# Adding a bias to the rows of a graph-attention table instead of to their weighted sums

## The chip, the cores and the metric

The kernel runs on one core of a Trainium2 chip. The metric is the device time of one execution in microseconds. The names of the engines are PE (matrix products; PEld is its loading of weights), DVE (vector), ACT (scalar and activation), POOL (GpSimd, which also issues the indirect gathers) and SP (which issues most of the other transfers).

## The reference

The reference applies a two-layer graph attention network (GAT) to 3125 nodes with 768 features and 53125 edges that are sorted by destination. Cut to what matters:

```python
h = relu(layernorm(x))                       # 3125 x 768
# layer 1: 4 heads of 256 columns
xl = h @ W1                                  # 3125 x 1024, the "table"
e  = leaky_relu((xl . a_src)[src] + (xl . a_dst)[dst])
alpha = softmax of e over the edges of one destination   # sums to 1 per node
out = segment_sum(xl[src] * alpha, dst) + b1
h1 = relu(layernorm(out) * g1 + be1) + h @ Wr1 + br1
# layer 2: the same with 1 head of 768 columns on h1, bias b2; result added to x
```

The attention logits come from `h` and folded weights, not from the stored table. The weights alpha of a node, with that of its own row in the table, add up to 1, so a constant that is added to each row of the table is found in each weighted sum once.

## The kernel before

**Tiling.** The nodes are worked in 25 blocks of 125 (`NB`, `P`). The edges of a block lie in a window of 18 groups (`J`) of 128 edges.

**Products of layer 1.** `products` (L636 to L654) multiplies each block by `w1` in two halves of 512 columns; ACT copies each half from PSUM to a tile `row` (L648; two buffers), and POOL's queue stores the row to the DRAM table `table1` (L146, L147: 112 and 13 rows). Each `yield` after three matmuls is a step that other code calls as filler, in an order that is written out by hand for PE, ACT and DVE. The loads of `x` tiles beyond the fourth go through the same POOL queue (L140), eight blocks ahead of their use.

**Softmax of layer 1.** `softmax` (L333 to L484) looks up the logits with one-hot matrices: per block DVE builds `ohd`, `le`, `ohs` and `ohh` (L375 to L382), PE multiplies `ohs` by small tables `tabs` (L392) and `ohd` by `tabd` (L400), and DVE multiplies and reduces the results (L394, L397, L402). The filler steps of `products` stand between them on PE. The small tables come from a split of the logits into three bfloat16 parts (`part`, `rest`). A scratch tile `scr`, in the place where later `wr1` lies, holds larger intermediates.

**Between softmax and sums.** PE ends the products and multiplies the first four blocks by `wr1` (L744). DVE folds the attention vectors of layer 2 into `wa2` from tiles `ab2`, `w2k` and `w2t` (L736, L737). Then the pools of the sums open in memory that earlier pools have left, and the first use of each tile waits for the last use of what lay there.

**Sums of layer 1.** `sums` (L486 to L571) gathers, for each block, 18 groups of 128 rows of 1024 columns by indirect DMA on POOL's queue (`g`, L525, ten buffers, so up to ten gathers ahead). ACT and DVE split each weighted row into two fp32r parts (`hi` L543, `g` L544), and PE sums them into `pa` through a one-hot matrix `oh` (L548); one group in 18 goes by another form (`w`, L558, L560). At the end of each block two matmuls of two rows (`ones_r` and `bias`, L564) add the bias, which was split into two fp32r parts beforehand by `split_biases` and loaded as `b1_r`. Between the groups PE takes steps of other work: residual products from `h0k` tiles (L777), and `end1` of the block before (L807, L820). Here a scheduler with its own estimates, not the hand, sets the order on the engines.

**Layer 2** goes through the same functions with one head and its own bias `b2`.

Of the kernel before, what the change touches and what calls it, by code (L numbers as in the profile page):

```python
# [9 lines left out]
F32 = mybir.dt.float32  # L10
F32R = mybir.dt.float32r
BF16 = mybir.dt.bfloat16
# [16 lines left out]
J = 18  # L29
# [29 lines left out]
def in_order(  # L59
# [42 lines left out]
    slo16_d = dram.tile([E], I16, name="slo16_d")  # L102
    keep_d = dram.tile([H * NB, S + 2], BF16, name="keep_d")

    parts_d = dram.tile([2, HC + 2 * C2], F32, name="parts_d")

    ident = const.tile([128, 128], F32, name="ident")
    make_identity(nc, ident)
# [45 lines left out]

    def split_biases(pool):

        for name, vec, plus, n, o in (("b1", b1, None, HC, 0), ("b2", b2, None, C2, HC), ("ball", br2, be2, C2, HC + C2)):
            v = pool.tile([128, n // 128], F32, name=name + "_v")
            nc.sync.dma_start(v, vec.rearrange("(p c) -> p c", p=128))
            if plus is not None:  # L160
                u = pool.tile([128, n // 128], F32, name=name + "_u")
                nc.sync.dma_start(u, plus.rearrange("(p c) -> p c", p=128))
                nc.vector.tensor_add(v, v, u)
            hi = pool.tile([128, n // 128], F32R, name=name + "_hi")
            nc.vector.tensor_copy(hi, v)
# [167 lines left out]
    def softmax(heads, asad, al, alo_d, pp, nq, ends=False, scr=None, fill=iter(()), side=None,  # L333
# [8 lines left out]
        with tc.tile_pool(name="so", bufs=1, side=side, reuse_waits=waits) as so:  # L342
            own = so.tile([128, J, V, NB], F32, name="own")
            if scr is not None:
                first = scr()
                n = J * heads * NB
                picks = [first[:, :n].rearrange("p (j h b) -> p j h b", h=heads, b=NB)]
                ohhs = [first[:, n + i * J * NB:n + (i + 1) * J * NB].rearrange("p (j b) -> p j b", b=NB)
                        for i in range(2)]
                le = first[:, n + 2 * J * NB:n + 2 * J * NB + S // 2].bitcast(BF16)  # L350
            with tc.tile_pool(name="sb", bufs=2, side=side, reuse_waits=waits) as sb:

                part = sb.tile([P, 3, NB * V], BF16, name="part", bufs=1)
                rest = sb.tile([P, NB * V], F32, name="rest", bufs=1)
                flat = asad.rearrange("p b v -> p (b v)")
                nc.vector.tensor_copy(part[:, 0, :], flat)
                nc.vector.tensor_sub(rest, flat, part[:, 0, :])
                nc.vector.tensor_copy(part[:, 1, :], rest)
                nc.vector.tensor_sub(part[:, 2, :], rest, part[:, 1, :])
                tabs = sb.tile([P, 3, heads, NB], BF16, name="tabs", bufs=1)  # L360
                tabd = sb.tile([P, NB, 3, V], BF16, name="tabd", bufs=1)
                for i in range(3):
                    v = part[:, i, :].rearrange("p (b v) -> p b v", v=V)
                    nc.vector.tensor_copy(tabs[:, i], v[:, :, :heads].rearrange("p b h -> p h b"))
# [51 lines left out]
            with tc.tile_pool(name="sr", bufs=1, side=side, reuse_waits=waits) as sr:  # L416
# [2 lines left out]
                bw = sr.tile([R, S], F32, name="bw")  # L419
                eo = sr.tile([128, J, heads, NB], F32, name="eo")  # L420
                m = sr.tile([128, J, heads, NB], F32, name="m")
                s = sr.tile([128, J, heads, NB], F32, name="s")
                keep = sr.tile([R, S + 2], BF16, name="keep")
                nc.sync.dma_start(keep, keep_d[:R, :])
                pen = sr.tile([R, S + 2], BF16, name="pen")
# [60 lines left out]
    def sums(heads, cols, table, al, alo_d, bias, split, ahead, his, lag, gp, pp, end, more=iter(())):  # L486
# [4 lines left out]
        f = width // 2  # L491
        n = min(cols, f)
        assert split(0) or n == f
        running = []

        def step():
# [19 lines left out]
        with tc.manual_schedule(engines={PE, ACT, DVE}) if lag else nullcontext():  # L516
            for b in range(NB):
                own = gp.tile([128, width], F32, name="own", bufs=3 if lag else 2)
                pa = pp.tile([P, 2, 512], F32, name="pa", bufs=2)
                ao = gp.tile([128, heads + 1], F32, name="ao", bufs=3)  # L520
                for j in range(J):
                    c = b * J + j
                    g = gp.tile([128, width], F32R, name="g", bufs=ahead)
                    gf = g.bitcast(F32)
                    nc.gpsimd.indirect_dma_start(  # L525
                        out=gf, out_offset=None, in_=table[:, :],
                        in_offset=bass.IndirectOffsetOnAxis(ap=idx_s[:, c:c + 1], axis=0))
                    if j == 6:
                        load_rows(nc.sync, own, table, b)
                    if j == 2:  # L530
                        nc.gpsimd.indirect_dma_start(
                            out=ao, out_offset=None, in_=alo_d[:, :],
                            in_offset=bass.IndirectOffsetOnAxis(ap=at_last[:, b:b + 1], axis=0))
                    if split(j) or heads > 1:
                        oh = gp.tile([128, 128], F32R, name="oh", bufs=max(his, 4) + 4)
                        nc.vector.tensor_scalar(oh, iota_f, rel_s[:, c:c + 1], None, op0=OP.is_equal)  # L536
                    if split(j):

                        hi = gp.tile([128, width], F32R, name="hi", bufs=his)
                        for h in range(heads):  # L540
                            cs = slice(h * cols, (h + 1) * cols)
                            a = al[:, j, h, b:b + 1]
                            nc.scalar.activation(hi[:, cs], gf[:, cs], AF.Copy, scale=a)  # L543
                            nc.vector.scalar_tensor_tensor(g[:, cs], gf[:, cs], a, hi[:, cs].bitcast(F32),  # L544
                                                           op0=OP.mult, op1=OP.subtract)
                        for t in (hi, g):
                            for i in range(2):
                                nc.tensor.matmul(pa[:, i, :f], oh[:, :P], t[:, i * f:(i + 1) * f],  # L548
                                                 start=(j == 0 and t is hi), stop=False)
# [12 lines left out]
                    if j == J - 1:  # L562
                        for i in range(2):
                            nc.tensor.matmul(pa[:, i, :f], ones_r, bias[:, i * f:(i + 1) * f],  # L564
                                             start=False, stop=True)
                    step()
                running.append(finish(b, own, pa, ao))
            while running:
                step()


    with tc.tile_pool(name="m1", bufs=1) as mp:
# [10 lines left out]
        with tc.tile_pool(name="w1", bufs=1) as wp, tc.tile_pool(name="pm1", bufs=1, space=PSUM) as pm1:  # L583
            w1 = wp.tile([128, NK1, HC], F32, name="w1")
            wa1 = wp.tile([128, NK1, 2 * H], F32, name="wa1")
            h0 = []
            with tc.tile_pool(name="d1", bufs=2) as dp, tc.tile_pool(name="pd1", bufs=1, space=PSUM) as pp:
                xts = {}

# [47 lines left out]
                def products():  # L637

                    for b in range(NB):
                        gi, o = b // GB, (b % GB) * P  # L640
                        row = wp.tile([P, HC], F32, name="row", bufs=2)
                        for i in range(2):
                            pm = pm1.tile([128, 512], F32, name="pm", bufs=3)
                            for k in range(NK1):
# [3 lines left out]
                                    nc.scalar.activation(row[:, i * 512:(i + 1) * 512], pm[:P], AF.Copy)  # L648
                                if k % 3 == 2:
                                    if i == 1 and k == NK1 - 1:  # L650
                                        store_rows(nc.gpsimd, table1, b, row)
                                        if gi and (b % GB == GB - 1 or b == NB - 1):
                                            nc.sync.dma_start(h0T_d[gi][:, :, :o + P], h0[gi])
                                    yield  # L654
# [59 lines left out]
                        next(fill)  # L714
            with tc.tile_pool(name="pq1", bufs=1, space=PSUM) as pp:
                softmax(H, asad1, al1, alo1_d, pp, 4, True,
                        lambda: mp.tile([128, 2 * S], F32, tag="wr1", name="scr"), fill=fill, steps=(3, 8, 2, 8, 2))
                br1_c = by_chunk(br1, mp, NK2, "br1_c")
                wr1 = mp.tile([128, NK1, HC], F32, tag="wr1", name="wr1")
                for k in range(NK1):  # L720
# [29 lines left out]
        with tc.tile_pool(name="w2", bufs=1, reuse_waits="tile") as wp, tc.tile_pool(name="e1", bufs=2, reuse_waits="tile") as ep, \  # L750
# [9 lines left out]

            for k in range(NK1):
                load(1, k)
            b1_r = bias_rows(wp, 0, HC, "b1_r")
            g1_c = by_chunk(g1, wp, NK2, "g1_c")
            be1_c = by_chunk(be1, wp, NK2, "be1_c")
            for k in range(NK2):
# [59 lines left out]
                        nc.vector.tensor_copy(asad2[:, b, :], pm[:, 384:n])  # L826
                store_rows(nc.sync, table2, b, row)

            sums(H, C1, table1, al1, alo1_d, b1_r, lambda j: j % 18 != 8, 10, 4, 0, gp, pp, end1, later())


    with tc.tile_pool(name="m2", bufs=1, reuse_waits="tile") as mp, \
            tc.tile_pool(name="pr2", bufs=1, space=PSUM, reuse_waits="tile") as pr:
        al2 = mp.tile([128, J, 1, NB], F32, name="al2")
        ball_r = bias_rows(mp, HC + C2, C2, "ball_r")
        FIRST = 9
        xrs = {}
        loaded = {}
# [60 lines left out]

        with tc.tile_pool(name="w3", bufs=1, reuse_waits="tile") as wp, tc.tile_pool(name="e2", bufs=2, reuse_waits="tile") as ep, \  # L900
                tc.tile_pool(name="g2", bufs=1, reuse_waits="tile") as gp, tc.tile_pool(name="pg2", bufs=1, space=PSUM, reuse_waits="tile") as pp:
            b2_r = bias_rows(wp, HC, C2, "b2_r")
            g2_b = wp.tile([P, C2], F32, name="g2_b")
            nc.sync.dma_start(g2_b, bcast(g2, C2))

# [483 lines left out]
```

## Time and profile before

| | us |
|---|---|
| median of 5 runs | 2362.45 (2352.91 to 2367.83) |
| the profiled execution, its own time | 2356.76 |
| span of its core | 2354.9 |
| PE, DVE, ACT, POOL busy | 2208.5, 1975.4, 1293.9, 1217.0 |

The span is cut into stages by the instructions in it: start and products (0 to about 225), softmax of layer 1 (225 to 464, with products until 468 and `wr1` products until 508), sums of layer 1 (508 to 1507), softmax of layer 2 (to about 1680), sums of layer 2 (to the end). In rows of the timeline the first number is the start, the second the duration or the stretch of several like instructions, and brackets hold the idle time before the first of them with what ended it. A float32 product is recorded as two matmuls, so a pair there is one instruction of the program.

### The profile page before, as it was taken

To read this page: it belongs to the slowest core of one execution; us is meant where nothing else is said; L and a number is where in the kernel's file an instruction comes from. 1 tells how busy PE (TensorE), PEld (TensorE's weight loads), DVE (VectorE), ACT (ScalarE), POOL (GpSimd) and SP (SyncE) were. 2 spreads that over 40 slices of the span, in tenths; PEclk is the share of its full clock that TensorE was granted. 3 is DMA by queue.
4 is the path that set the end of the run, shared out by engine and by line. 5 is a ranking of instruction groups with operands and counts; after the bars stand their busy time and mean duration, and the time that the engine had idled before them with its cause. 6 is when DMAs were issued, how large, how long until landed. Compare 5 with 4: busy or idle time off the path is not lost. (4 is left out here: it accounts for less than half of the span.)

```text
span 2354.9 us, 35889 instructions
## 1 busy us (share of the span) xinstructions
PE 2208.5 (94%) x11154; PEld 1439.7 (61%) x11154; DVE 1975.4 (84%) x4429; ACT 1293.9 (55%) x2687; POOL 1217.0 (52%) x1043
## 2 busy tenths in 40 slices
PE   5898999989999999999999999799999999999996
PEld 2466665446666666666666765466566676666664
DVE  6845999769999999898989999588678788788877
ACT  1231332229988888888888999100244444444443
POOL 2100000027766766566766676000377777777775
PEclk8998999999999999999999999799999999999998
DMA  5453552379998898988988988687499999998996
GB/s 186 154 195 98 187 191 81 114 249 386 326 323 305 294 336 294 312 312 302 324 294 295 337 316 298 232 290 253 154 311 337 322 329 314 329 322 308 305 307 216
DMA packets 185691, 637.97 MB, mean 271 GB/s; under 512 B 32170, under 2 KB 49435, under 8 KB 184724
## 3 DMA queue, kind: packets, MB, share of 16 engines
q0 software_dynamic: 109072, 437.23, 54.1%
q1 hardware_dynamic: 72570, 188.75, 22.9%
q10 hardware_dynamic: 3850, 9.60, 1.1%
q8 instruction: 93, 1.52, 0.3%
q14 instruction: 106, 0.87, 0.1%
HBM read 567.40 MB, written 68.08 MB: 270 GB/s over the span
## 5 line engine op out<-in xcount | busy, mean ns | idle before, releaser
L525 POOL DMA_INDIRECT g<-table,idx_s x900 | 1110.0, 1233 | 464.6 <-PE pa L548 264.2
L543 ACT ACTIVATE hi<-g,al 128x256 fp32r<-128x256 f32 (+1 forms) x2025 | 1008.8, 575 | 462.1 <-DMA g<-table,idx_s 267.5
L544 DVE SCALAR_TENSOR_TENSOR g<-g,al,hi 128x256 fp32r<-128x256 f32 (+1 forms) x2025 | 1033.0, 560 | 125.8 <-ACT hi L543 123.8
L548 PE MATMUL pa<-hi,oh 128*125 128x512 f32 (+1 forms) x1500 | 602.5, 481 | 23.4 <-DVE oh L536 14.2
L548 PE MATMUL pa<-g,oh 128*125 128x512 f32 (+1 forms) x1500 | 472.5, 390 | 22.0 <-DVE g L544 21.9
L548 PEld LDWEIGHTS pa<-hi,oh 128*125 128x125 f32 x1500 | 274.8, 189 | 215.1 <-issue 66.2
L548 PEld LDWEIGHTS pa<-g,oh 128*125 128x125 f32 x1500 | 272.2, 187 | 101.2 <-DVE g L544 58.1
L820 PE MATMUL p<-w,h1T 128*125 128x384 f32 (+1 forms) x800 | 300.1, 494 | 1.8 <-DVE h1T L811 1.5
L854 PE MATMUL pr<-wr,h 128*125 128x384 f32 x800 | 296.6, 503 | 3.1 <-DMA h<-h1T_d 3.1
L645 PE MATMUL pm<-w,h 128*125 128x512 f32 x600 | 281.1, 618 | 0.0
L777 PE MATMUL pr<-h0k,wr 128*128 128x500 f32 (+1 forms) x576 | 257.4, 536 | 8.9 <-DMA h0k<-h0T_d 8.1
L536 DVE TENSOR_SCALAR oh<-iota_f,rel_s 128x128 fp32r<-128x128 f32 x775 | 208.0, 280 | 58.4 <-PE pa L548 58.4
L560 PE MATMUL pa<-g,w 128*125 128x384 f32 (+1 forms) x700 | 234.3, 463 | 5.1 <-ACT w L558 4.1
L854 PEld LDWEIGHTS pr<-wr,h 128*125 128x125 f32 x800 | 151.0, 193 | 86.2 <-issue 14.4
L820 PEld LDWEIGHTS p<-w,h1T 128*125 128x125 f32 x800 | 148.5, 188 | 81.4 <-issue 10.8
L146 POOL DMA_DIRECT2D table<-row x25 | 16.0, 640 | 348.4 <-ACT row L648 321.3
L645 PEld LDWEIGHTS pm<-w,h 128*125 128x125 f32 x600 | 112.9, 196 | 125.3 <-issue 124.0
L560 PEld LDWEIGHTS pa<-g,w 128*125 128x125 f32 x700 | 129.4, 189 | 70.2 <-ACT w L558 12.4
L777 PEld LDWEIGHTS pr<-h0k,wr 128*128 128x128 f32 x576 | 104.5, 191 | 51.9 <-ACT hi L543 6.5
L392 PEld LDWEIGHTS <-ohs 125*128 125x128 bf16 x2700 | 101.6, 98 | 47.9 <-DVE ohs L380 32.9
L392 PE MATMUL pq<-tabs,ohs 125*128 125x100 bf16 (+1 forms) x2700 | 105.2, 193 | 22.3 <-DVE ohs L380 20.5
L648 ACT ACTIVATE row<-pm 125x512 f32<-125x512 f32 x50 | 29.8, 595 | 149.3 <-PE pm L645 138.4
(198 smaller groups left out, 1683.2 us busy)
## 6 DMA issues: line engine op xcount, KB each, us to landing
bd<-dst_d SPq DMA_DIRECT2D x50, 576.0 KB
bs<-slo_d SPq DMA_DIRECT2D x50, 576.0 KB
g<-table,idx_s POOLq DMA_INDIRECT x900, 5.9
r1T_d<-rt SPq DMA_DIRECT2D x100, 125.0 KB
r1t<-r1T_d SPq DMA_DIRECT2D x25, 500.0 KB
h1T_d<-h1T SPq DMA_DIRECT2D x25, 500.0 KB
h<-h1T_d SPq DMA_DIRECT2D x25, 500.0 KB
own<-table SPq DMA_DIRECT2D x24, 512.0 KB
```

The source lines that it names most:

```text
L392: nc.tensor.matmul(q[:, j], ohs[:P, (j0 + j) * 128:(j0 + j + 1) * 128], tabs[:, i], start=(i == 0), stop=(i == 2))
L525: nc.gpsimd.indirect_dma_start(out=gf, out_offset=None, in_=table[:, :], in_offset=bass.IndirectOffsetOnAxis(ap=idx_s[:, c:c + 1], axis=0))
L536: nc.vector.tensor_scalar(oh, iota_f, rel_s[:, c:c + 1], None, op0=OP.is_equal)
L543: nc.scalar.activation(hi[:, cs], gf[:, cs], AF.Copy, scale=a)
L544: nc.vector.scalar_tensor_tensor(g[:, cs], gf[:, cs], a, hi[:, cs].bitcast(F32), op0=OP.mult, op1=OP.subtract)
L548: nc.tensor.matmul(pa[:, i, :f], oh[:, :P], t[:, i * f:(i + 1) * f], start=(j == 0 and t is hi), stop=False)
L560: nc.tensor.matmul(pa[:, o // f, o % f:o % f + n], w[:, o // cols, :], gf[:, o:o + n], start=(j == 0), stop=False)
L645: nc.tensor.matmul(pm[:P], h0[gi][:, k, o:o + P], w1[:, k, i * 512:(i + 1) * 512], start=(k == 0), stop=(k == NK1 - 1))
L648: nc.scalar.activation(row[:, i * 512:(i + 1) * 512], pm[:P], AF.Copy)
L777: nc.tensor.matmul(pm[:, :nb * P], wr1[:, k, m * 128:(m + 1) * 128], loaded[gi, k][:, :nb * P], start=(k == 0), stop=(k == NK1 - 1))
L820: nc.tensor.matmul(pm[:, :n], hT[:, k, :], w2[:, k, o:o + n], start=(k == 0), stop=(k == NK2 - 1))
L854: nc.tensor.matmul(pm[:, :384], h1[:, k, :], wr2[:, k, i * 384:(i + 1) * 384], start=(k == 0), stop=False)
```

## The change

The bias `b1` is loaded once, at the start, by ACT's queue as a tile `b1_b` of 125 equal rows. POOL adds it to each finished `row` before the row is stored to `table1`. The two matmuls of the bias at the end of each block of layer 1's sums go, and with them the preparation and the load of `b1_r`. To make room, `part`, `rest` and `tabd` of layer 1's softmax move into the scratch tile, and `s` shares the buffer of `m`.

```diff
-        for name, vec, plus, n, o in (("b1", b1, None, HC, 0), ("b2", b2, None, C2, HC), ("ball", br2, be2, C2, HC + C2)):
+        for name, vec, plus, n, o in (("b2", b2, None, C2, 0), ("ball", br2, be2, C2, C2)):
...
+                if scr is not None:
+                    part = first[:P, n:n + 3 * NB * V // 2].bitcast(BF16).rearrange("p (i v) -> p i v", i=3)
+                    n += 3 * NB * V // 2
+                    rest = first[:P, n:n + NB * V]
+                    n += NB * V
+                    tabd = first[:P, n:n + 3 * NB * V // 2].bitcast(BF16).rearrange(
+                        "p (b i v) -> p b i v", i=3, v=V)
...
-                s = sr.tile([128, J, heads, NB], F32, name="s")
+                s = m
...
-                                                 start=(j == 0 and t is hi), stop=False)
+                                                 start=(j == 0 and t is hi),
+                                                 stop=(bias is None and j == J - 1 and t is g))
...
-                    if j == J - 1:
+                    if bias is not None and j == J - 1:
...
+            b1_b = wp.tile([P, HC], F32, name="b1_b")
+            nc.scalar.dma_start(b1_b, bcast(b1, HC))
...
                                     if i == 1 and k == NK1 - 1:
+                                        nc.gpsimd.tensor_add(row, row, b1_b)
                                         store_rows(nc.gpsimd, table1, b, row)
...
-                        lambda: mp.tile([128, 2 * S], F32, tag="wr1", name="scr"), fill=fill, steps=(3, 8, 2, 8, 2))
+                        lambda: mp.tile([128, NK1 * HC], F32, tag="wr1", name="scr"), fill=fill, steps=(3, 8, 2, 8, 2))
...
-            b1_r = bias_rows(wp, 0, HC, "b1_r")
...
-            sums(H, C1, table1, al1, alo1_d, b1_r, lambda j: j % 18 != 8, 10, 4, 0, gp, pp, end1, later())
+            sums(H, C1, table1, al1, alo1_d, None, lambda j: j % 18 != 8, 10, 4, 0, gp, pp, end1, later())
```

What the two built programs differ in: on PE 50 instructions are gone and the order of the rest is kept but for the first and the last two blocks of the sums; POOL has 25 more, in four of the first blocks with a load of `x` between the addition and its two stores; SP has four transfers fewer and ACT's queue one more; DVE has two fewer. The places of tiles in on-chip memory also move. Before, the ten `g` buffers of layer 1 lie at bytes 137728 to 178688 of each partition and `ab2` at 172032 to 178176; after, `g` lies at 133536 to 174496 and `ab2` at 176032 to 182176. The second gather of layer 1 waits, before, for the last DVE instruction of the fold that reads `ab2`; after, for the last product of `products`.

More of the change, by code (lines that the diff above doesn't have):

```diff
@@ L103, in in_order @@
     keep_d = dram.tile([H * NB, S + 2], BF16, name="keep_d")
-    parts_d = dram.tile([2, HC + 2 * C2], F32, name="parts_d")
+    parts_d = dram.tile([2, 2 * C2], F32, name="parts_d")
     ident = const.tile([128, 128], F32, name="ident")
@@ L349, in softmax @@
                         for i in range(2)]
-                le = first[:, n + 2 * J * NB:n + 2 * J * NB + S // 2].bitcast(BF16)
+                n += 2 * J * NB
+                le = first[:, n:n + S // 2].bitcast(BF16)
+                n += S // 2
             with tc.tile_pool(name="sb", bufs=2, side=side, reuse_waits=waits) as sb:
-                part = sb.tile([P, 3, NB * V], BF16, name="part", bufs=1)
-                rest = sb.tile([P, NB * V], F32, name="rest", bufs=1)
+                if scr is not None:
[5 more added lines that the diff above has]
+                        "p (b i v) -> p b i v", i=3, v=V)
+                else:
+                    part = sb.tile([P, 3, NB * V], BF16, name="part", bufs=1)
+                    rest = sb.tile([P, NB * V], F32, name="rest", bufs=1)
+                    tabd = sb.tile([P, NB, 3, V], BF16, name="tabd", bufs=1)
                 flat = asad.rearrange("p b v -> p (b v)")
@@ L360, in softmax @@
                 tabs = sb.tile([P, 3, heads, NB], BF16, name="tabs", bufs=1)
-                tabd = sb.tile([P, NB, 3, V], BF16, name="tabd", bufs=1)
                 for i in range(3):
@@ L493, in sums @@
         assert split(0) or n == f
+        assert split(J - 1)
         running = []
@@ L834, in in_order @@
         al2 = mp.tile([128, J, 1, NB], F32, name="al2")
-        ball_r = bias_rows(mp, HC + C2, C2, "ball_r")
+        ball_r = bias_rows(mp, C2, C2, "ball_r")
         FIRST = 9
@@ L901, in in_order @@
                 tc.tile_pool(name="g2", bufs=1, reuse_waits="tile") as gp, tc.tile_pool(name="pg2", bufs=1, space=PSUM, reuse_waits="tile") as pp:
-            b2_r = bias_rows(wp, HC, C2, "b2_r")
+            b2_r = bias_rows(wp, 0, C2, "b2_r")
             g2_b = wp.tile([P, C2], F32, name="g2_b")
```

## The prediction

> **What bounds the kernel now.** I read the page's table of 40 slices first, then the windows view over the stages that the change touches, the PE timeline of one block of the sums, the timeline of the turn from softmax to sums, and DVE and POOL side by side in the softmax.
>
> Busy time by stage, from the windows view (stretch, length, then busy time and instructions of PE, PEld, DVE, ACT, POOL, then clock, DMA share, GB/s):
>
> ```profile
> core 0: us, PE busy (x) PEld busy (x) DVE busy (x) ACT busy (x) POOL busy (x), PEclk, DMA share, GB/s
> 240.00:300.00 60.00, 56.57 (x681) 37.48 (x679) 60.00 (x84) 21.09 (x22) 4.68 (x6) 1.00 0.57 182
> 826.85:866.49 39.64, 39.64 (x143) 25.65 (x142) 36.35 (x100) 34.10 (x86) 27.56 (x19) 1.00 0.94 337
> 600.00:1300.00 700.00, 698.12 (x2501) 451.46 (x2500) 643.54 (x1782) 602.70 (x1502) 468.67 (x339) 1.00 0.90 309
> ```
>
> The sums of layer 1 are bound by PE: it idles 1.9 of 700 us at full clock, while DVE has 3.3 us to spare in a block of 39.64. The softmax of layer 1 is bound by DVE, which idles not at all in 240 to 300, with PE close behind. So the change takes work from the bound of one stage, and puts work beside the bound of another.
>
> One block's end on PE, with the bias pair and, later, the same three neighbours without it:
>
> ```profile
> 826.29 0.63 PE L548 MATMUL pa<-g,oh 128*125 128x512 f32 x2
> 826.85 0.72 PE L564 MATMUL pa<-b_r,ones_r 2*125 2x512 f32 x2
> 827.50 1.56 PE L820 MATMUL p<-w,h1T 128*125 128x384 f32 x4
> 828.60 0.92 PE L548 MATMUL pa<-hi,oh 128*125 128x512 f32 x2
> ...
> 849.25 0.62 PE L548 MATMUL pa<-g,oh 128*125 128x512 f32 x2
> 849.71 1.46 PE L820 MATMUL p<-w,h1T 128*125 128x384 f32 x4
> 850.71 0.92 PE L548 MATMUL pa<-hi,oh 128*125 128x512 f32 x2
> ```
>
> Durations overlap here, so starts are compared: from the start of `g` to the start of the next `hi` it is 2.31 us with the pair and 1.46 without. The pair costs 0.85 us.
>
> The turn to the sums (POOL's gathers; then what PE waits for):
>
> ```profile
> 477.18 1.01 POOL L525 DMA_INDIRECT g<-table,idx_s  x1 [7.36 <-issue]
> 502.63 0.96 POOL L525 DMA_INDIRECT g<-table,idx_s  x1 [24.44 <-DMA r1T_d<-rt]
> ...
> 513.78 3.67 PE L777 MATMUL pr<-h0k,wr 128*128 128x500 f32 x4 [5.68 <-DMA h0k<-h0T_d]
> 521.19 1.11 PE L777 MATMUL pr<-h0k,wr 128*128 128x500 f32 x2 [2.46 <-DMA h0k<-h0T_d]
> ```
>
> The second gather stands still for 24.44 us. The profile names a transfer; the program's waits name the fold of `wa2` on DVE, whose last product starts near 501. Then nine gathers and the loads of `h0k` go out together, the DMA engines are full (share 1.01 in 510 to 520), and PE idles 8.1 us for `h0k`.
>
> DVE and POOL beside each other in the softmax:
>
> ```profile
> 304.13 0.81 DVE L380 TENSOR_SCALAR ohs<-bs,node_f 128x2304 bf16<-128x2304 int16 x1
> 304.32 0.73 POOL L146 DMA_DIRECT2D table<-row  x1 [19.43 <-ACT row L648]
> 304.85 0.62 DVE L382 TENSOR_TENSOR scr<-iota_f,hi_s 128x450 f32<-128x450 f32 x1
> ```
>
> The store's issue takes 0.73 us here, and 0.99 to 1.19 at 245.60, 263.39, 283.21 and 341.67, against 0.53 to 0.54 at 321.85 and 380.31, where DVE is in reductions or in products from PSUM. POOL is held up by some DVE instructions, so the two get in each other's way.
>
> **The bias pair goes.** 24 blocks by 0.85 us, and the first, where no L820 stands behind the pair (551.82 to 553.03, 1.21 against 0.47), 0.75: 21.1 us, all on PE's path. The next limit is near: a block of 38.8 us leaves DVE 2.4 and ACT 4.7, and gathers wait mostly for PE to free buffers (264.2 us by the page). I take 20, between 17 and 21.
>
> **The turn to the sums.** Unasked, the new layout lets gathers 2 to 10 go from about 480 on instead of 502.63, while the DMA engines have room (share 0.62 in 450 to 500). ACT still copies the last residual at 508.13 and takes the first `hi` at 508.71, so nothing starts sooner there; but the loads of `h0k` meet emptier queues, and the first of them no longer waits for PE's last L744. What can go is the 8.1 us of PE idle. What is late next: the second `h0k` load, still issued by SP near 511, and DVE, which needs about 1.87 us for a group (four L544 at 0.41, one `oh` at 0.21). Against it, nine gathers of 512 KB beside the fold's `w2k` loads can hold the fold up; it has 4 us before 508.71. I take 6 off, between 0 and 8.
>
> **The addition on POOL.** 25 instructions of 125x1024 with two inputs; no row shows one. From below, DVE's add of two inputs takes 2026 ns for 1800 columns (L460): 1.15 us for 1024. From above, POOL's nearest row:
>
> ```profile
> masks.py:199 POOL TENSOR_SCALAR_AFFINE_SELECT ident<-ident 128x128 f32<-128x128 f32 x1 | 0.3, 284 | 0.0
> ```
>
> 284 ns for 128 columns, in proportion 2.27 us for 1024. I take the upper, the same engine's. The Trainium skill, "GPSIMD Engine Reference", section "Performance versus the Vector engine", gives 4497 ns for such an add over 2048 columns; half of it is an estimate of 2.25 us, which no run here has shown yet.
>
> As POOL's own time, 25 by 2.27 is hidden: rows come at least 9 us apart and POOL idles 321.3 us for them. Behind the addition its two stores and, early, one load of `x` are queued; the loads are eight blocks ahead, else PE's transposes would wait 2.3 us each. The buffer of `row` is wanted again two blocks later, 20 us at the densest, against 0.6 + 2.3 + 3.8 (landing). The last store goes near 471 instead of 468.78 and the first gather 2.3 us later; ACT needs it only at 508.71.
>
> What is not hidden is what DVE loses. If DVE never waits, 0. If an addition shuts out every DVE instruction that either runs fast on 2304 columns or reads two tiles, I lay 2.27 us at each of the 25 times of L146 over DVE's timeline: between 240 and 410, where each DVE delay moves PE too, six of nine additions block for 2.2 to 2.3 us (245.60, 263.39, 283.21, 304.32, 341.67, 362.78) and two more beside the scans (394.75, 405.06): 18.2 us. With 1.15 us it is 9.3. From 421 to 442 PE is late instead (DVE waits 5.8 us for it at 443), which hides two more. I take 12, nearer to the upper end, since the store issues show the meeting at just these six places, but the phases will shift as PE gains time.
>
> The Trainium skill speaks against this part: "SBUF — State Buffer", section "Who interferes with whom", has DVE and GpSimd share one pair of ports under a lock for the whole instruction, where the second "fully blocks". By it the term would be 18 and the total 6 us higher; the trace shows only POOL as the one that waits.
>
> **The rest.** Before 225 ten additions meet a DVE with gaps: 1, from 0 to 3. The load of `b1_b` (500 KB, at the best slice's 386 GB/s 1.3 us) joins the start, where DVE waits 11.21 us for small bias loads until 32.20; one of these goes: 1, from -1 to 3. SP's four fewer transfers lie where SP is not waited for. `part`, `rest`, `tabd`, and `s` in `m` keep DVE's order, and the scratch tile's next writer comes after PE's last `tabd` product anyway: nothing, and if that order failed, one PE product of 0.6 us.
>
> **Sum.** -20 - 6 + 12 + 1 + 1 = -12 on the profiled execution's 2356.76, so 2344.8. That execution lies 5.7 below the median 2362.45; the median goes to 2350. A measurement of this kernel can tell about 0.5% from no change, 11.8 us; my sum lies just beyond.
>
> **Rivals.** (a) DVE does not wait; POOL alone does, as the store issues show. Then -24: 2338. (b) DVE is blocked in full and the turn gives nothing, because the fold is held up or DVE's pace replaces the idle: -20 + 18 + 2 = 0, 2362. For it: DVE has no idle to absorb anything there. (c) Slower: POOL's two reads follow each other at the one-input row's price, 4.5 us an addition. Over the same timeline this blocks DVE for 38 us between 240 and 410; with -26 and +2 it makes +14, 2376. It decides from about 3.0 us an addition on (24 us of blocking cancel the gain). Against it: 284 ns must contain a fixed part, since a POOL fill of 128x1 already takes 0.10. (d) PE is not the true bound of the sums, since its ends are modelled, and the pair's time goes to waits for DVE: half the gain, 2360. Against it: PE's groups of starts add up without gaps.
>
> **Numbers.** Forecast 0.45, (a) 0.22, (b) 0.20, (c) 0.08, (d) 0.05. The forecast's own range, 2344 to 2356, lies on both sides of the bound, half and half. Faster by over 0.5%: 0.23 + 0.22 = 0.45; within: 0.22 + 0.20 + 0.05, less 0.02, 0.45; slower: (c) and 0.02 for unseen costs on top of the worst sum of bounds (-17 + 18 + 3 + 3 = +7, 2369), 0.10. The best sum is -21 - 8 + 0 + 0 - 1 = -30, 2332. Range 2334 to 2366: it leaves out (c) and the edges of (a) and (b).
>
> **What would show it.** Right: a block of the sums of 38.8 us; the second gather near 480; no 5.68 us before the first L777; DVE rows of L375 to L382 stretched, or gaps before them, beside each POOL addition of about 2.3 us; and the last L744 ending near 522 instead of 508. Wrong: blocks still near 39.6, additions over 3 us, or `al` (L397) ending at the same time as before.

## The result, and the profile after

The changed kernel takes 2373.15 us (median of 42 runs, 2364.88 to 2384.79), against 2363.30 for the kernel before (79 runs on the same chips). The ratio is 1.0043, with a 95% interval of 1.0035 to 1.0051: about 10 us slower, where 12 us faster was predicted. The profiled execution took 2371.62 us with a span of 2369.8. That of before (2356.76) lies 6.5 below the median of its 79 runs, so the two spans differ by 14.9 where the medians differ by 10; below, what the price of a part is comes from ratios times 2363, and what it is made of comes from traces.

Busy time by stage, after, from the windows view (columns as in the prediction; the one block of the sums is 39.00 long):

```profile
240.00:300.00 60.00, 52.81 (x605) 34.11 (x604) 60.00 (x79) 18.99 (x20) 8.28 (x9) 1.00 0.57 183
827.00:866.00 39.00, 39.00 (x142) 25.48 (x141) 36.46 (x102) 33.74 (x86) 27.77 (x21) 1.00 0.97 361
600.00:1300.00 700.00, 699.65 (x2527) 457.62 (x2526) 656.75 (x1825) 614.64 (x1550) 457.89 (x349) 1.00 0.90 317
```

In the softmax DVE is still busy all the time, but in 60 us it now gets through 79 instructions instead of 84, and PE through 605 instead of 681: DVE is not idle, it is slow. In the sums PE is the bound as before.

The end of two blocks on PE, after, from the timeline:

```profile
827.53 0.62 PE L560 MATMUL pa<-g,oh 128*125 128x512 f32 x2
827.99 1.46 PE L836 MATMUL p<-w,h1T 128*125 128x384 f32 x4
...
866.34 0.62 PE L560 MATMUL pa<-g,oh 128*125 128x512 f32 x2
866.80 1.46 PE L836 MATMUL p<-w,h1T 128*125 128x384 f32 x4
```

The pair is gone from between `g` and the products of L836, and the same place comes round after 38.81 us, against 39.64 before.

The turn on POOL, and what PE waits for there, after:

```profile
500.71 2.35 POOL L667 TENSOR_TENSOR row<-row,b_b 125x1024 f32<-125x1024 f32 x1 [6.59 <-ACT row L664]
...
511.91 1.61 POOL L537 DMA_INDIRECT g<-table,idx_s  x1 [7.50 <-issue]
513.83 0.96 POOL L537 DMA_INDIRECT g<-table,idx_s  x1 [0.30 <-issue]
515.10 0.94 POOL L537 DMA_INDIRECT g<-table,idx_s  x1 [0.31 <-issue]
```
```profile
541.43 1.92 PE L793 MATMUL pr<-h0k,wr 128*128 128x500 f32 x4 [1.20 <-DMA h0k<-h0T_d]
```

The second gather no longer stands still (it starts 1.92 us behind the first, where before it was 25.45), and PE's first wait for `h0k` is 1.20 us instead of 5.68. But the last row of the table is added only at 500.71; ACT's first `hi` comes at 541.6, against 508.7 before. Stage 1 (all that lies before the first `hi`) has lost 33 us, where the prediction had 14.

Where: POOL and DVE beside each other, after, from their timelines:

```profile
299.54 2.79 POOL L667 TENSOR_TENSOR row<-row,b_b 125x1024 f32<-125x1024 f32 x1 [17.97 <-ACT row L664]
```
```profile
297.57 2.01 DVE L407 TENSOR_REDUCE al<-scr 128x72 f32<-128x1800 f32 x1
299.51 0.61 DVE L392 TENSOR_TENSOR scr<-iota_f,hi_s 128x450 f32<-128x450 f32 x1
300.04 2.91 DVE L385 TENSOR_SCALAR ohd<-bd,node_f 128x2304 bf16<-128x2304 int16 x1
302.87 1.25 DVE L404 TENSOR_TENSOR scr<-pq,scr 128x500 f32<-128x500 f32 x2
```

L385 takes 0.81 us alone and 2.91 here: it ends 0.6 us after the addition, much as if it had begun behind it. DVE stays "busy" in the table, so no idle time and no wait shows this; only the mean of a group does, or one row beside another engine's. The groups of DVE in 240 to 400, before (the other two of its kind stood at 809 ns there) and then after:

```profile
L375 DVE TENSOR_SCALAR ohd<-bd,node_f 128x2304 bf16<-128x2304 int16 x19 | 15.4, 811 | 0.0
```
```profile
L385 DVE TENSOR_SCALAR ohd<-bd,node_f 128x2304 bf16<-128x2304 int16 x21 | 23.4, 1112 | 0.0
L390 DVE TENSOR_SCALAR ohs<-bs,node_f 128x2304 bf16<-128x2304 int16 x20 | 20.4, 1021 | 0.0
L387 DVE TENSOR_SCALAR scr<-bd,node_f 128x2304 bf16<-128x2304 int16 x19 | 18.2, 960 | 0.0
```

And the addition itself, from its group on the page and from the view of its line (min, median and max in ns):

```profile
L667 POOL TENSOR_TENSOR row<-row,b_b 125x1024 f32<-125x1024 f32 x25 | 66.1, 2645 | 314.1 <-ACT row L664 308.4
```
```profile
L667 POOL TENSOR_TENSOR row<-row,b_b x25: 2339/2349/4534, 46.4 to 500.7; 125x1024 f32<-125x1024 f32 x25
```

Alone it takes 2.35 us. That is what the prediction used (2.27).

### The profile page after: what moved, and what is told of

The parts are those of the page before. It is cut to its first block, busy times and chain, and to the rows that moved or that the text cites. A ratio compares the mean times of both kernels' runs of the same rounds, so it can differ in the third digit from the quotient of the medians.

```text
span 2369.8 us, 35878 instructions
## 1 busy us (share of the span) xinstructions
PE 2201.4 (93%) x11104; PEld 1436.8 (61%) x11104; DVE 2006.0 (85%) x4427; ACT 1286.8 (54%) x2687; POOL 1260.8 (53%) x1068
## 5 line engine op out<-in xcount | busy, mean ns | idle before, releaser
L537 POOL DMA_INDIRECT g<-table,idx_s x900 | 1088.9, 1210 | 444.4 <-PE pa L560 267.4
L836 PE MATMUL p<-w,h1T 128*125 128x384 f32 (+1 forms) x800 | 296.9, 489 | 2.4 <-DVE h1T L827 1.5
L667 POOL TENSOR_TENSOR row<-row,b_b 125x1024 f32<-125x1024 f32 x25 | 66.1, 2645 | 314.1 <-ACT row L664 308.4
L836 PEld LDWEIGHTS p<-w,h1T 128*125 128x125 f32 x800 | 149.8, 188 | 76.0 <-DVE h1T L827 3.9
L573 PEld LDWEIGHTS pa<-g,w 128*125 128x125 f32 x700 | 129.7, 190 | 72.3 <-ACT w L571 13.5
L402 PE MATMUL pq<-tabs,ohs 125*128 125x100 bf16 (+1 forms) x2700 | 106.3, 193 | 35.5 <-DVE ohs L390 33.7
```

The lines of the kernel that those rows point to most:

```text
L402: nc.tensor.matmul(q[:, j], ohs[:P, (j0 + j) * 128:(j0 + j + 1) * 128], tabs[:, i], start=(i == 0), stop=(i == 2))
L537: nc.gpsimd.indirect_dma_start(out=gf, out_offset=None, in_=table[:, :], in_offset=bass.IndirectOffsetOnAxis(ap=idx_s[:, c:c + 1], axis=0))
L667: nc.gpsimd.tensor_add(row, row, b1_b)
L836: nc.tensor.matmul(pm[:, :n], hT[:, k, :], w2[:, k, o:o + n], start=(k == 0), stop=(k == NK2 - 1))
```

## The experiments

**The theory** (T1): an addition on POOL holds something that many of DVE's instructions need, so that the two exclude each other, and DVE sets the pace of the softmax of layer 1. **Rivals**: R1, the load of `b1_b` and POOL's queue delay stage 1, and DVE's longer rows are harmless; R2, the sums give back less than thought.

To measure T1's cause by itself I use DVE's extra time: for each DVE row up to the first `hi`, what it lasts beyond the median of the rows of the same source line and shape in the trace of before, where that is over 0.15 us. It doesn't move with PE's clock or with when a stage starts. The first four kernels below (none, half, twice, and the places in memory) ran on a chip where the kernel before takes 2411.80 us, with a longer layer 2; their ratios are to that.

### How much is added

No addition:

```diff
-                                        nc.gpsimd.tensor_add(row, row, b1_b)
```

> The changed kernel without its 25 additions on POOL; b1 is still loaded to all partitions at the start, but nothing adds it, so layer 1 lacks its bias. Theory T1 (an addition on POOL shuts out the DVE instructions that lie beside it, and DVE sets the pace of the softmax of layer 1): DVE's L385 group returns from a mean of 1.11 us to 0.81, the last row copy of layer 1 (32 us later than before in the changed kernel) is only 3 to 6 us later, and the time lies about 19 us under the kernel before: -17 for the bias pair, -7 for the turn, +5 for the start; ratio 0.992. Rival R1 (the delay comes from the load of b1 at the start and from queues, DVE's stretching is harmless): stage 1 stays 25 us or more late and the ratio stays at 1.00 to 1.004. Rival R2 (the sums give back less than thought): stage 1 recovers but the ratio is no lower than 0.997.

Measured: 0.9913 (0.9886 to 0.9940). Half of the columns:

```diff
-    nc.gpsimd.tensor_add(row, row, b1_b)
+    nc.gpsimd.tensor_add(row[:, :512], row[:, :512], b1_b[:, :512])
```

> The changed kernel with the addition on the first 512 of the 1024 columns only, so half of b1 is left out. T1 (blocking in proportion to the length of an addition): additions of about 1.2 us, DVE blocked by half: stage 1 ends about 13 us earlier than in the changed kernel, ratio about 0.998. If the cost of a meeting is fixed (a lock taken once for each addition, whatever its length): no lower than 1.002. R1 (load and queues): within 2 us of the changed kernel, ratio 1.003 to 1.005.

Measured: 0.9959 (0.9943 to 0.9974). Twice:

```diff
     nc.gpsimd.tensor_add(row, row, b1_b)
+    nc.gpsimd.tensor_add(row, row, b1_b)
```

> The changed kernel with every addition done twice in a row, so layer 1's bias counts twice. T1: 25 more additions of 2.35 us right behind the first ones; each blocks DVE about as much as the first, stage 1 ends 20 to 30 us later than in the changed kernel and the ratio is 1.013 to 1.017. R1 (POOL's additions are hidden): ratio 1.004 to 1.006.

Measured: 1.0115 (1.0086 to 1.0143). And, in a later round, where it is added:

```diff
-                                        nc.gpsimd.tensor_add(row, row, b1_b)
+                                        if b < 9:
+                                            nc.gpsimd.tensor_add(row, row, b1_b)
```

> The changed kernel with the additions on POOL for the first 9 of 25 row blocks only (those done before the softmax, where DVE idles more than half of the time); the other 16 blocks lack b1. T1 with the place as the cause (an addition costs only where DVE has no idle time): the 9 early ones cost 2 to 8 us, the 16 left out give back 23 to 29 of the 31, ratio 0.992 to 0.9945, near the 0.9913 without any addition. If an addition costs the same anywhere (about 31/25 us): 11 us of additions left, ratio 0.996 or more.

Measured: 0.9936 (0.9914 to 0.9958). All five together, the time as ratio less 1, times 2363:

| additions | us against before (interval) | DVE's extra time, us | DVE rows with extra time |
|---|---|---|---|
| none | -20.6 (-26.9 to -14.2) | 0.0 | 0 |
| first 9 rows | -15.1 (-20.3 to -9.9) | 9.0 | 8 |
| 25 half rows | -9.7 (-13.5 to -6.1) | 10.6 | 11 |
| 25 rows (the change) | +10.2 (+8.3 to +12.1) | 33.8 | 21 |
| 25 rows twice | +27.2 (+20.3 to +33.8) | 50.9 | 31 |

From none to all, DVE's extra time rises by 33.8 us and the time by 30.8 (24 to 37 by the two intervals). The 16 later additions alone bring 24.8 us of extra time and 25.3 us of time by the ratios, 21 by the medians, and 22.1 at the last row copy of the two traces (500.0 against 477.9); the nine early ones 9.0 and 5.5, the latter with an uncertainty of 8. So T1 holds: between 0.8 and 1 us is paid for each us of extra time where DVE has no idle time. R1 falls as the account of the 31 us: its load is in the kernel without additions too, and that is the fastest of the five. R2 falls, since its ratio could not be under 0.997. A cost that is fixed for each meeting falls as well, since half rows stay far under its 1.002: there a DVE row is held for 1.07 us at most, beside a whole addition for 2.14. In size the steps are uneven: the half rows cost less than I had expected (10.9 us over none, not half of 31), and the second addition of a pair 17 us, a little under the range given. The extra time is as uneven (10.6 and 17.1), since the number of rows that are held changes too.

One sign of T1 came only in part: without additions the last row copy is 10.2 us later than before (478.1 against 467.9), where T1 had 3 to 6 and R1 25 or more, and with nine additions it is 10.0 later. Six kernels that have neither an addition in stage 1 nor the load at its start have it at 469.5 to 474.1, so 2 to 6 us of this are there without either. What makes them was not tried.

In the kernel with nine additions those nine last what the prediction took, and DVE's rows in 240 to 400 are as before:

```profile
L668 POOL TENSOR_TENSOR row<-row,b_b 125x1024 f32<-125x1024 f32 x9 | 21.2, 2359 | 83.5 <-ACT row L664 83.5
```
```profile
L385 DVE TENSOR_SCALAR ohd<-bd,node_f 128x2304 bf16<-128x2304 int16 x20 | 16.4, 820 | 0.0
```

### The load at the start

```diff
-            nc.scalar.dma_start(b1_b, bcast(b1, HC))
...
                             abs1 = folded(mp, H, C1, a_src1, a_dst1, "wr1", 2)
+                        if b == 3:
+                            nc.gpsimd.dma_start(b1_b, bcast(b1, HC))
```

> The changed kernel, whole, with the load of b1 to all partitions taken out of the start and issued on POOL's queue at the fourth row block, after the first loads of x and the weights. The first row copies should then come as early as in the kernel before. If the load at the start is what delays the start (5 us at the first row copy and 8 us by 200 us in the kernel without additions, against the kernel that only moves own), the time falls by 5 to 9 us against the changed kernel: ratio to the kernel before 1.0005 to 1.002. If the delay at the start comes from the additions or from the chip's clock: ratio 1.003 to 1.005.

Measured: 1.0025 (1.0010 to 1.0040), so about 4 us less than the changed kernel. The value lies between the two that were expected, the interval reaches into both, and it just overlaps that of the changed kernel: the price is 0 to 8 us. In the traces the load's mark is on SP's queue, where the next pair of loads of `x` is issued in 6.20 us with the load at the start and in 0.83 without (the changed kernel, then this one):

```profile
3.52 6.20 SPq L140 DMA_DIRECT2D xt<-in_x_dram  x2
```
```profile
3.09 0.83 SPq L140 DMA_DIRECT2D xt<-in_x_dram  x2
```

The first row copies did not come earlier by as much, though (45.3 against 45.7 us in the two profiles), and the first `hi` did not either (542.8 against 541.6). In the other kernels that don't load `b1_b` there the first row copies came at 42.0 to 46.1, so single profiles can't resolve this part; the price rests on the ratios alone.

### Each part alone

The places in memory alone: in the kernel before, `own` is taken after the other tiles of the sums.

```diff
-                own = gp.tile([128, width], F32, name="own", bufs=3 if lag else 2)
+                own = gp.tile([128, width], F32, name="own", bufs=3) if lag else None
...
                     if j == 6:
+                        if own is None:
+                            own = gp.tile([128, width], F32, name="own", bufs=2)
```

> The kernel before, whole, with one thing moved: in layer 1's sums the tile own is taken after the others, so that the gathered tiles g end below the place of ab2, as they do in the changed kernel. It tells what the turn to the sums is worth alone. My sum's term: the second gather goes out at about 480 instead of 502.6 and up to 8 us of PE's waiting for h0k goes, total 5 to 8 us less, ratio 0.997. Rival: the early gathers only take the transfers' room from the fold of wa2 and ACT's first hi sets the start anyway, ratio 0.999 to 1.001; the 7 us seen in the changed kernel then came from its late stage 1, after which the fold's loads had long landed.

Measured: 0.9979 (0.9960 to 0.9998), 5 us less. From ACT's first `hi` to the last copy of `row2` the layer takes 989.8 us in this trace, against 996.9 in that of before. Its gathers:

```profile
478.82 1.71 POOL L525 DMA_INDIRECT g<-table,idx_s  x1 [7.39 <-issue]
480.84 0.96 POOL L525 DMA_INDIRECT g<-table,idx_s  x1 [0.30 <-issue]
482.10 0.94 POOL L525 DMA_INDIRECT g<-table,idx_s  x1 [0.30 <-issue]
```

So the turn's gain is real, of the predicted size, and comes from where `g` lies, as `ab2` lies above it: the second gather goes out at 480.84 instead of 502.63.

The small tables in the scratch tile and `s` in `m`, alone (the rest as before):

```diff
-                part = sb.tile([P, 3, NB * V], BF16, name="part", bufs=1)
-                rest = sb.tile([P, NB * V], F32, name="rest", bufs=1)
+                if scr is not None:
+                    part = first[:P, n:n + 3 * NB * V // 2].bitcast(BF16).rearrange("p (i v) -> p i v", i=3)
...
-                s = sr.tile([128, J, heads, NB], F32, name="s")
+                s = m
```

> The kernel before with only the second part of the change: the small tables of the lookups in the scratch tile and s in m. No addition, the bias pair kept, the gathered tiles where they were. The prediction took this part at nothing: ratio 0.9985 to 1.0015, layer 2 (from the last row2 copy to the end) 844 to 852 us as in the kernels with the old places. Rival: it costs some 5 us in layer 2, where five profiled runs with the new places took 853 to 857: ratio 1.002 or more, layer 2 at 853 or more.

Measured: 0.9995 (0.9975 to 1.0014). Layer 2 took 852.8 us in its trace, and yet the time is that of before, so the rival is not borne out; the interval leaves it 3 us at most. It is not settled by the traces. In ten profiles of kernels on chips with equal times the same layer took 843.8 to 851.2 us in the four with the old places and 852.6 to 857.0 in the six with the new, without an overlap; but three of those four executions lie 4 to 7 us under the median of their kernel, so much of the gap can be spread between executions.

### The addition elsewhere

On DVE, to `z`, in the kernel before without the pair:

```diff
+            b1_b = wp.tile([P, HC], F32, name="b1_b")
+            nc.sync.dma_start(b1_b, bcast(b1, HC))
...
+                nc.vector.tensor_add(z, z, b1_b)
                 yield from norm_steps(ep, z, HC)
```

> The kernel before, its places in memory kept, without the bias pair; b1 is loaded to all partitions with the other constants of the sums and DVE adds it to z after the sums of a block (1.15 us estimated from the 2026 ns for 1800 columns). T1 with the sums bound by PE: the pair's 17 to 20 us go, DVE's 36.4 us of a block become 37.5 of 38.8 and are hidden, nothing is blocked in stage 1: ratio 0.992 to 0.9935. Rival (d) of the prediction (PE is not the true bound of the sums, DVE's time follows): no gain, 0.998 to 1.003.

Measured: 0.9998 (0.9981 to 1.0016). This missed: I expected 15 to 19 us less. With `own` moved as well, by the same edit as under "Each part alone":

> The kernel with the addition to z on DVE, and own taken after the other tiles of the sums, so that the early gathers need not wait for the fold. If both gains are real and add: 17 to 20 for the pair and 5 for the turn, ratio 0.989 to 0.992, the fastest so far. If the turn's gain in the layout run was chance: as the run without it.

Measured: 0.9972 (0.9958 to 0.9985), a miss too: 19 to 26 us less were expected, and it is 7. And with `b1` loaded in the fourth row block, into a tile of the pool `m1`, instead of at the turn (and the small tables in the scratch tile, which makes the room):

```diff
+        b1_b = mp.tile([P, HC], F32, name="b1_b")
...
+                        if b == 3:
+                            nc.gpsimd.dma_start(b1_b, bcast(b1, HC))
...
-            b1_b = wp.tile([P, HC], F32, name="b1_b")
-            nc.sync.dma_start(b1_b, bcast(b1, HC))
```

> The whole computation, a candidate: the addition to z on DVE and own after the other tiles, as in the run before of that kind, but b1 is loaded early, in the fourth row block, into a tile that lives through layer 1, so its 500 KB no longer meet the crowded turn. There the first block of the sums ended 5 us later than in the run that only moves own. If the load did that: ratio 0.993 to 0.9955. If DVE's addition itself did (1.21 us in a stretch where PE waits for DVE's products right after the end of a block): 0.9965 to 0.998 as before.

Measured: 0.9934 (0.9909 to 0.9959), which is 15.6 us less, 10 to 21 by the interval; the medians, 2354.0 and 2364.0 us, are 10.0 apart. This version is faster than both kernels. Its addition costs half of POOL's (the group in 700 to 1300):

```profile
L814 DVE TENSOR_TENSOR z<-z,b_b 125x1024 f32<-125x1024 f32 x16 | 19.5, 1216 | 0.0
```

The three differ in the first block: from the first `hi` to the first copy of `row2` they take 91.6, 82.4 and 76.2 us, where the kernel before takes 82.7 and the one with `own` moved 77.1. Two gains are there: the second goes with the place of `g`, the third with 500 KB less to move at the turn (or with the small tables' places, which this kernel changes too). What they have in common fits the rest of the miss: a block with residuals takes mostly 39.0 us, not 38.8, and two near the end, which have none, 36.6 and 36.8 against 36.1 and 36.3 before, and 35.4 and 35.5 in the changed kernel. There, I take it, DVE sets the pace, and its 1.22 us count; this was not tried apart.

On POOL, to `z`:

```diff
-                nc.vector.tensor_add(z, z, b1_b)
+                nc.gpsimd.tensor_add(z, z, b1_b)
                 yield from norm_steps(ep, z, HC)
```

> As the kernel with the addition to z on DVE, but POOL adds. It puts the same addition (2.35 us alone, 25 times) beside the sums, where DVE idles 2.4 us a block of 38.8, in place of beside the softmax, where DVE idles not at all. T1: DVE's L544 of two tiles is stretched by 2 to 4.5 us a block, DVE's slack covers most of it, ratio 0.993 to 0.999, between the DVE variant and the kernel before, DVE's L544 mean up by about 20 to 60 ns over its 81 calls a block. If the place of the additions doesn't matter: 22 us lost as in stage 1, ratio 1.001 or more. A further cost may be gathers queued behind an addition that waits for z; with 10 buffers of g, I expect none.

Measured: 1.0140 (1.0117 to 1.0164), 33 us slower, far outside what T1 gave, and on the side of the rival by which the place of the additions doesn't matter (1.001 or more). A block takes 40.4 us. Its waits of PE, and DVE's largest group, both in 700 to 1300:

```profile
PE pa L548 <- DVE g L544: 11.4, 43, 0.4
```
```profile
L544 DVE SCALAR_TENSOR_TENSOR g<-g,al,hi 128x256 fp32r<-128x256 f32 x1006 | 449.0, 501 | 0.0
```

L544 takes 501 ns on average instead of 473, about 1.9 us a block over its 67 calls in the window. That is the stretch I expected, but I let DVE's 2.4 us of slack in a block absorb it. It doesn't: PE now waits for `g` 43 times, a few tenths of a us each, which in 700 to 1300 of before it never did. Slack that lies in other places of the block is of no use to the group that stands beside the addition. How much of the rest is due to POOL's gathers, which queue behind an addition that waits for `z`, was not tried apart.

On PE, in stage 1: the first nine rows by POOL, the other 16 by the pair, in the products of the table.

```diff
                                 nc.tensor.matmul(pm[:P], h0[gi][:, k, o:o + P], w1[:, k, i * 512:(i + 1) * 512],
-                                                 start=(k == 0), stop=(k == NK1 - 1))
+                                                 start=(k == 0), stop=(k == NK1 - 1 and b < 9))
+                                if k == NK1 - 1 and b >= 9:
+                                    nc.tensor.matmul(pm[:P], ones_r, b1_r[:, i * 512:(i + 1) * 512],
+                                                     start=False, stop=True)
```

> The whole computation, a candidate: the first 9 row blocks get b1 by POOL's addition, the other 16 by the bias pair on PE, but in the products of layer 1's table beside the softmax, where DVE sets the pace, not in the sums. 19 for the pair gone from the sums and 5 for the turn, less 2 to 8 for the early additions, 3 for the four blocks that PE makes after the softmax, and 0 to 10 for 12 pairs of 0.85 us that PE, with some 12 us idle between 240 and 420, has to fit in: ratio 0.990 to 0.997. If PE is as late as DVE in the softmax, so that every pair counts: 0.9965 or more.

Measured: 0.9978 (0.9964 to 0.9993), above the range given and where the rival has it (0.9965 or more, every pair counts): 10 us more than the kernel that adds in nine rows only. Its windows view of the softmax, after that of the kernel with nine additions:

```profile
240.00:420.00 180.00, 171.55 (x1792) 108.22 (x1791) 177.88 (x234) 58.05 (x65) 14.43 (x20) 1.00 0.47 156
```
```profile
240.00:420.00 180.00, 177.00 (x1815) 108.62 (x1812) 176.35 (x234) 57.52 (x64) 12.27 (x18) 1.00 0.47 155
```

PE goes from 171.55 to 177.00 of 180 us busy: its idle time there was too small for the pairs, 16 of which make 13.6 us at 0.85. The last row copy comes 12.8 us later (490.7 against 477.9).

## Why the prediction was wrong

By its own steps:

**The bound of each stage**: right. Blocks of the sums follow PE, the softmax follows DVE.

**The bias pair, -20**: right in the mechanism, and 0.85 us in each block with residuals. From the first to the last copy of `row2` the three kernels with the pair and no other work in the sums take 912.7 to 914.2 us; the changed kernel takes 897.4 and six variants with its sums 896.2 to 904.1. So 24 blocks give 9 to 18, mostly 13 to 17, somewhat under the sum's 20; single blocks differ by 2 us between executions, and the rest was not resolved.

**The turn, -6**: right. 5 by the ratio of the layout alone, 7 by the traces.

Both together, from the first `hi` to the last copy of `row2`: 971.9 us, against 996.9, so -25 where the sum has -26.

**The additions on POOL, +12 and +1**: this is the step that failed; by the ratios they cost 31 (24 to 37). The duration was right, 2.35 for 2.27, and so were the places. The sum laid an addition at each store of before between 240 and 410. There are ten of them, not nine: eight meetings, which make its 18.2, and two stores without one. What the addition to the same row did in the changed kernel:

| store before, at | addition after, at | in the sum's 18.2 | DVE row held, and by how much, us |
|---|---|---|---|
| 245.60 | 257.42 | yes | L387, 1.07 |
| 263.39 | 277.86 | yes | L387, 1.89 |
| 283.21 | 299.54 | yes | L385, 2.10 |
| 304.32 | 322.77 | yes | L390, 2.12 |
| 321.85 | 342.45 | no | none |
| 341.67 | 362.25 | yes | L385, 2.10 |
| 362.78 | 386.15 | yes | L390, 2.12 |
| 380.31 | 405.83 | no | L182, 2.07 |
| 394.75 | 424.04 | yes | L465, 2.11 |
| 405.06 | 434.34 | yes | L467, 2.14 |

Together 17.7 us. All eight meetings took place, and a ninth that was not in the sum made up for the two that were short. The full blocking of 18.2 was the right figure, and 12 the wrong choice: the phases were to shift, but no meeting was lost. All of it came on the path. Against the kernel with nine additions, the row copies are later by 1.3 us at the tenth row and by 22.1 at the twenty-first, which is 20.8 for the 19.9 us of extra time of the eleven additions in between (these ten, and the tenth row's at 237.14, which held L385 by 2.13).

- From 421 to 442 of before the sum had PE late, which hides two more. That was right: the additions at 457.94 and 468.25 hold L481 by 2.10 and L484 by 2.04, and one at 490.42 holds L488 by 2.06, but the row copies stay 22.1 later to the last.
- "Before 225 ten additions", at 1 in the sum: the tenth alone held L385 by 2.13, and is in the 20.8. The nine before it bring 7.7 us of extra time here and 9.0 in the kernel that has only these; 5.5 count by the two ratios, with an uncertainty of 8, and in the traces the last row copy comes at the same time with them as without any (477.9 and 478.1).

So the traces show the two terms at 20 to 23 us (last row copy and first `hi`, against the kernels with nine additions and with none), where the sum had 13, and the ratios at 31. What lies between the two was not found; the ratios' uncertainty is as large.

**The load of `b1_b`, +1**: about 4 by the late load, with 0 to 8 open.

Put together, by parts measured apart: -25 for the sums and the turn and +4 for the load make -21, against -20.6 without additions, and 31 for the additions make the measured +10. The two profiles, 14.9 apart, divide in another way: stage 1 +32.9 (the sum had 14), from the first `hi` to the last copy of `row2` -25 (it had -26), layer 2 +7.1 (it had nothing). Of stage 1's loss, by the last row copies, 22 us are the 16 later additions, and 10 are there with nine additions or none. Some 5 us of the 14.9 come from the spread of the two executions about their medians.

**The rivals.** (a) falls: DVE waits. (b) had the full blocking right, and was wrong that the turn gives nothing. (c) has the nearest time, 2376, by another way, so that is luck: it needed 4.5 us an addition, and alone one takes 2.35. (d) falls for the changed kernel, where blocks went from 39.64 to 38.8; DVE becomes the bound only when it is given the addition as well.

The step taken with least reason was the choice of 12, "nearer to the upper end", because the trace of before showed only POOL as the one that waits. The Trainium skill's page "SBUF — State Buffer", section "Who interferes with whom", which the prediction weighed and put at 18, describes what was measured: one of the two engines has the shared ports for its whole instruction and the other waits. L385 goes from 0.81 to 2.91 us beside an addition, and L404, which reads one tile from PSUM, keeps its 0.67. The prediction laid it over its ten additions, got 18, and then took a third off. With the 18, against 17.7 measured, its sum would have been -6: nearer, but still without the sign, which the other terms (the early additions, the load, and what the two runs leave open) have to bring.

## What to carry to other kernels

Before work is moved to an idle engine, ask which of the bound engine's instructions can't run beside it, lay the moved instructions over its timeline, and where it has no idle time charge the whole of what they hold up: here that came to 17.7 us for ten additions, where full blocking gave 18.2 and 12 was allowed. All 25 additions of 2.35 us, on an engine idle most of the time, cost about 31 us. Blocking doesn't show as a wait or as idle time; compare the mean duration of the same group before and after. A bias that is cheap for PE in a place where PE is the bound is worth moving only where the other engine has time at that very place: added to `z` on DVE, with its load kept out of the crowded turn, with the gathers of the turn freed, it came to 10 to 21 us less (0.9934), of which the freed gathers alone give about 5.

## What was not expected of the hardware

POOL waits as well. Beside the first scan and the second one, after:

```profile
424.04 4.23 POOL L667 TENSOR_TENSOR row<-row,b_b 125x1024 f32<-125x1024 f32 x1 [14.50 <-ACT row L664]
```
```profile
421.18 4.95 DVE L464 TENSOR_TENSOR_SCAN scr<-pen,scr 100x2304 f32<-100x2304 bf16 x1
426.04 7.04 DVE L465 TENSOR_TENSOR_SCAN bw<-pen,scr 100x2304 f32<-100x2304 bf16 x1
```

The addition comes during L464, which keeps its 4.95 us; it ends 4.23 us later, 2.1 after the end of that scan, and L465 takes 7.04 us where it took 4.93. Whoever is first goes on, the other waits, in turns. So the group's mean of 2645 ns holds waiting of POOL's own.

And a short DVE instruction is held as well: this one, of 25 columns, took 0.17 us in the trace of before and is held for 2.07, as long as the large ones:

```profile
405.98 2.24 DVE L182 TENSOR_SCALAR ult<-upto 128x25 f32<-128x25 f32 x1
```
